# Where P1 + P6 is built in the layer-1 scores of a two-layer attention kernel

## The chip, the cores and the metric

The kernel runs on one core of a Trainium2 chip. A core has TensorE (matmuls, "PE" in the profile; its weight loads are "PEld"), VectorE ("DVE"), ScalarE ("ACT"), GpSimd ("POOL") and SyncE ("SP", which here only issues DMAs). Matmul results land in PSUM, everything else lies in SBUF. The metric is the device time of the launch in microseconds, the median of several runs.

## What is computed

Eight images of 512 channels by 1024 tokens go through two attention layers, all in float32. Layer 0 has eight heads. Layer 1 has one head over all 512 channels, and the change lies in its scores. Cut to that, the reference reads:

```python
xn = group_norm(x, gamma, beta)
q = conv1x1(xn, q_w, q_b).reshape(b, c, h * w).transpose(0, 2, 1)
k = conv1x1(xn, k_w, k_b).reshape(b, c, h * w)
v = conv1x1(xn, v_w, v_b).reshape(b, c, h * w).transpose(0, 2, 1)
attn = jax.nn.softmax(jnp.einsum('bqc,bck->bqk', q, k) * scale, axis=-1)
out = jnp.einsum('bqk,bkc->bqc', attn, v)
```

## The kernel before

**Stages.** The work is traced in Python as one straight program. For each image b from 1 on it does: layer 0's attention for b (`attention0`), the projection of b (`projection`, which also makes a list `stats` of twelve deferred statistics operations for layer 1's norm), then layer 1 of image b - 1: `layer1_scores` (the query side g), `layer1_rest` with `scores1_twice` (scores and exponentials), the values z and the product with the values (`values1`), and then layer 0's values, keys and queries of image b + 1. The last image's layer 1 takes another routine, `scores1`. So `scores1_twice` runs seven times.

**The scores as a fast matrix product, twice over.** In `scores1_twice` the 1024 x 1024 scores are split into 2 x 2 blocks C11, C12, C21, C22 and computed with Winograd's form of Strassen's scheme: seven products P1 to P7 in place of eight, and

- C11 = P1 + P2
- U2 = P1 + P6, U3 = U2 + P7
- C12 = U2 + P5 + P3, C21 = U3 + P4, C22 = U3 + P5

Each product is computed by the same scheme again (`inner_steps`): seven inner steps in the order 1, 6, 2, 5, 7, 3, 4. An inner step is two matmuls of 128 x 128 weights by 256 columns; in float32 the profile shows four matmul records for it. Three PSUM banks a, b and c (two buffers each, so `psa`, `psb`, `psc` in the profile) hold the inner sums. Step 1 fills bank a, and ScalarE copies it into a new bank b (L459). Steps 6, 7 and 4 accumulate onto b, step 2 onto a, step 5 opens c and step 3 accumulates onto it. Between two accumulations onto the same bank, a partial sum is read out: u2 after step 6, c5 after step 5, the inner block (1,1) after step 7. VectorE does this reading with `add` (L720: PSUM plus an SBUF block into SBUF), or ScalarE with a copy (L449) where the product has nothing to add. So VectorE must have read a bank before TensorE may do the next step on it.

Steps 3 and 4 of a product are put off (`tail`) and are done after step 1 of the next product. Within a product the inner blocks are written in the order (0,0) by step 2, (1,1) by step 7, (0,1) by step 3, (1,0) by step 4.

**The seven products.** `product(s, p, y, x, before, small, after7, final)` is called in the order P1, P2, P5, P6, P7, P3, P4. It computes Pp, adds the block at place `x` (if any) and writes to place `y`; (0,1) is C12, (1,0) is C21, (1,1) is C22. `before` names the products whose query-side factors GpSimd builds at that point (`factors`, `query_factors`, four operations each, L426). `small` is a list of deferred operations that is appended to `background`; one of them is taken off after each inner step. They are: `gsteps`, sums of the query side on VectorE (L159 to L162); `stats`, eight `bn_stats` (L98) and four `bn_aggr` (L103) on VectorE; and `add_up`, sums of exponentials for the softmax on GpSimd (L731). `exps` are the exponentials in place on ScalarE (L727), two per block. `final` and `after7` put `exps` behind the last or the fifth inner step.

**The extra sums.** C22 holds P5 after the third product. U2 = P1 + P6 is written to C12's place; P7 reads U2 there and writes U3 to C21's place. In P7's product, `extra` (L746 to L752) then calls `more` (L722) twice for each inner block: when P7's add has read U2's block, C12 += C22 there (so C12 = U2 + P5), and when U3's block is written, C22 = U3 + P5. Six of these eight sums run on GpSimd, two on VectorE: C12's inner block (0,1) and C22's inner block (1,0). All are line L723, 128 x 512.

**What sets the order.** Each engine works off its own queue in order. A planner in the framework orders the instructions of each queue when the program is built; it may move an instruction ahead of others on its engine, while those wrapped in `tc.keep_in_program_order` keep their order among themselves. Matmuls, the factors on GpSimd (L426), `add_up` and `stats` are wrapped so; `add` and the old `more` are not. The framework also puts in all the waits, and it takes a buffer from a common pool of 32 tiles when a tile is first written.

Of the kernel before, what the change touches and what calls it, by code (L numbers as in the profile page):

```python
# [12 lines left out]
ALU = mybir.AluOpType  # L13
# [16 lines left out]
def two_attention_blocks_kernel(  # L30
# [8 lines left out]
    nc = tc.nc  # L39
# [26 lines left out]
    def matmul(*args, **kw):  # L66
        tc.keep_in_program_order(nc.tensor.matmul(*args, **kw))  # L67
# [97 lines left out]
    def right_sums(lo, hi, t124, sub):  # L165

        n = len(lo)
        t1, t2, t4 = ([f(j) for j in range(n)] for f in t124)
        b11, b12, b21, b22 = [l[0] for l in lo], [l[1] for l in lo], [h[0] for h in hi], [h[1] for h in hi]
        steps = [lambda j=j: sub(t1[j], b12[j], b11[j]) for j in range(n)]  # L170
        steps += [lambda j=j: sub(t2[j], b22[j], t1[j]) for j in range(n)]
        steps += [lambda j=j: sub(b12[j], b22[j], b12[j]) for j in range(n)]
        steps += [lambda j=j: sub(t4[j], b21[j], t2[j]) for j in range(n)]
        return {1: b11, 2: b21, 3: b22, 4: t4, 5: t1, 6: t2, 7: b12}, steps

    def main_path(ctx):
# [11 lines left out]
        def pair_tile(name):  # L188
            return big_tile(name, (P, 2, HT))
# [226 lines left out]
        def query_factors(f, uid):  # L416

            t = big_tile(f"inner_{uid}", (P, 4, 2 * P))
            s1, s2, s3, s4 = (t[:, i, :] for i in range(4))
            a11, a21, a12, a22 = (f[k][:, ts(i, 2 * P)] for k in range(2) for i in range(2))  # L420
            for dst, x, y, op in (
                (s1, a21, a22, ALU.add), (s2, s1, a11, ALU.subtract), (s3, a11, a21, ALU.subtract),
                (s4, a12, s2, ALU.subtract),
            ):

                tc.keep_in_program_order(nc.gpsimd.tensor_tensor(dst, x, y, op))  # L426
            return {1: a11, 2: a12, 3: s4, 4: a22, 5: s1, 6: s2, 7: s3}
# [273 lines left out]
        def scores1_twice(b, f, gf, gsteps, first, uid, stats):  # L701

            scale = C**-0.5
            e = {(c, cc, r): pair_tile(f"e_{uid}_{c}{cc}{r}") for r in range(2) for c in range(2) for cc in range(2)}
            total = pair_tile(f"sum_{uid}")
            parts = [pair_tile(f"sum{r}_{uid}") for r in range(2)]  # L710
            g2 = {1: first}

            def factors(p):
                g2[p] = query_factors(gf[p], f"{p}_{uid}")

            def blocks(at, r, cc):
                return [e[at[1], cc, at[0]][:, :, ts(r, 2 * P)]]

            def add(dst, ps, x):
                nc.vector.tensor_add(dst[0], ps, x[0])  # L720

            def more(engine, dst, x, y, r, cc):  # L722
                engine.tensor_tensor(blocks(dst, r, cc)[0], blocks(x, r, cc)[0], blocks(y, r, cc)[0], ALU.add)  # L723

            def exps(r, c):
                for cc in (1, 0):
                    nc.scalar.activation(e[c, cc, r], e[c, cc, r], AF.Exp, scale=scale)  # L727

            def add_up(r, c):

                on = lambda dst, x, y: lambda: tc.keep_in_program_order(nc.gpsimd.tensor_tensor(dst, x, y, ALU.add))  # L731
                if r == c:
                    return [on(parts[r], e[c, 0, r], e[c, 1, r])]
                return [
                    *(on(parts[r], parts[r], e[c, cc, r]) for cc in range(2)),
                    on(total[:, r, :], parts[r][:, 0, :], parts[r][:, 1, :]),
                ]

            def product(s, p, y, x, before, small, after7=(), final=()):
                def mm(ps, j, start):  # L740
                    for i in range(2):
                        matmul(
                            ps[:, i, :], f[p][j][:, ts(i, P)], g2[p][j], start=start and i == 0, stop=True, skip_group_check=True
                        )

                def extra(r, cc, read, written):  # L746
                    if p == 7:

                        if read:
                            more(nc.vector if (r, cc) == (0, 1) else nc.gpsimd, (0, 1), (0, 1), (1, 1), r, cc)  # L750
                        if written:
                            more(nc.vector if (r, cc) == (1, 0) else nc.gpsimd, (1, 1), (1, 0), (1, 1), r, cc)  # L752

                inner_steps(
                    f"{uid}_{s}", s % 2, 2, mm, add, lambda *at: blocks(y, *at), x and (lambda *at: blocks(x, *at)),
                    extra, after7, final, [lambda: background.extend(small), *(lambda q=q: factors(q) for q in before)],
                )

            product(0, 1, (1, 0), None, [2], stats[:3] + gsteps[:2])
            product(1, 2, (0, 0), (1, 0), [5], gsteps[2:4], (), [lambda: exps(0, 0)])  # L760
            product(2, 5, (1, 1), None, [6, 4], gsteps[4:])
            product(3, 6, (0, 1), (1, 0), [7, 3], add_up(0, 0) + stats[3:6])
            product(4, 7, (1, 0), (0, 1), [], stats[6:7])
            product(5, 3, (0, 1), (0, 1), [], stats[7:10], [lambda: exps(1, 1)], [lambda: exps(0, 1)])
            product(
                6, 4, (1, 0), (1, 0), [], stats[10:] + add_up(1, 1) + add_up(0, 1), (),
                [lambda: exps(1, 0), lambda: background.extend(add_up(1, 0) + steps)],
            )

            t = [[pair_tile(f"t{n}_{uid}_{cc}") for cc in range(2)] for n in (1, 2, 4)]  # L770
            engines = [nc.vector] * 4 + [nc.gpsimd] * 4
            fs, steps = right_sums(
                [(e[0, cc, 0], e[0, cc, 1]) for cc in range(2)], [(e[1, cc, 0], e[1, cc, 1]) for cc in range(2)],
                [lambda cc, n=n: t[n][cc] for n in range(3)],
                lambda *a: engines.pop(0).tensor_tensor(*a, ALU.subtract),
            )
            return total, {p: [x[:, i, :] for x in fs[p] for i in range(2)] for p in fs}
# [167 lines left out]
        def projection(b, af, xt, hooks=()):  # L945

            norm = GroupNorm(1, f"1_{b}", pinned=b > 0)
            stats, rest = [], []

            def residual(i, r, c, ps, u):  # L950
                oc = 2 * r + i
                xh = xt[oc][:, ts(c, HT)]

                tc.keep_in_program_order(
                    nc.vector.scalar_tensor_tensor(xh, ps, obias[0][:, oc : oc + 1], xh, ALU.add, ALU.add)
                )
                if (r, c) == (1, 1):

                    rest.append(lambda: tc.keep_in_program_order(nc.vector.tensor_add(xh, xh, u)))
                elif u is not None:  # L960
                    nc.vector.tensor_add(xh, xh, u)
                stats.append(lambda: norm.half_stats(oc, c, xh))

                if c == 1 - r:
                    stats.append(lambda: norm.end_stats(oc))

            def add_rest():
                for f in rest:
                    f()

            def store():
                spills[b] = spool.tile([KC, P, T], F32, tag="spill", name=f"spill_{b}")
                for c in range(KC):
                    nc.sync.dma_start(spills[b][c], xt[c])

            by_channel(
                weight("p"), af, f"p_{b}", residual, middle=(5, 6, 7, 2), hooks=[[], [], hooks, [], [add_rest]],
                after=[load_weight, store],
            )
            return norm, stats  # L980
# [69 lines left out]
        for b in range(B):  # L1050
# [33 lines left out]
            if b > 0:  # L1084
# [4 lines left out]
                norm1, stats = projection(b, af, xt, [scaled, steps[7]])  # L1089
                gf, gsteps = layer1_scores(b - 1, hf, inner)  # L1090
# [12 lines left out]
            elif B > 1:  # L1103
                v, f, norm0 = values(1, hf, [[], [], [], [], [*steps[:7], scaled, steps[7]]])
                norm1, stats = projection(0, af, xt)
# [3 lines left out]
            else:  # L1109
# [3 lines left out]
                norm1, stats = projection(0, af, xt)  # L1113
# [9 lines left out]
        gf, gsteps = layer1_scores(B - 1, hf, None)  # L1123
# [197 lines left out]
```

## Time and profile before

| | |
|---|---|
| median of 3 runs | 2895.41 us |
| lowest and highest run | 2894.38, 2897.06 us |
| the profiled execution, its own time | 2894.85 us |
| its span, first to last instruction | 2893.1 us |
| TensorE busy | 2847.5 us |
| VectorE, ScalarE, GpSimd busy | 2069.1, 919.8, 1092.1 us |
| mean granted TensorE clock over the span | 0.997 |

In the lines of the profile, "psc<-inner,h" is an operation that writes tile psc from tiles inner and h; "128x512 f32" is partitions by elements; "L720" is line 720 of the kernel; "x4" means that four instructions are merged into one line; and brackets give the time for which the engine had been idle before and what ended it. Times are microseconds from the span's start. A matmul's end is modelled, so starts are what to read.

### The profile page before, as it was taken

The numbers are of one execution on the slowest core, as the hardware profiler recorded it, in microseconds if no ns is written. First come the engines' busy times: TensorE is split into PE (matmuls) and PEld (weight loads), VectorE is DVE, ScalarE is ACT, GpSimd is POOL, SyncE is SP. The second block draws the span as 40 slices with busy tenths as digits, with TensorE's granted clock in tenths as the row PEclk, the third lists the DMA queues.
The fourth block names the chain that finished last, engine by engine and source line by source line (L and its number), as shares of the span: only waits on it lengthen the run. The fifth ranks groups of instructions, "written<-read, shape, count | busy, mean of one in ns | idle before, by whom it ended". The sixth has DMA issues, their size and how long they took to land.

```text
span 2893.1 us, 31974 instructions
## 1 busy us (share of the span) xinstructions
PE 2847.5 (98%) x11720; PEld 1669.2 (58%) x11720; DVE 2069.1 (72%) x2732; ACT 919.8 (32%) x1166; POOL 1092.1 (38%) x1096
## 2 busy tenths in 40 slices
PE   9999999999999999999999999999999999999998
PEld 5435636765367653667437674376733768347544
DVE  5587787667876678775787757877588775886654
ACT  1351452214522045221542215421163212633110
POOL 2113216632166322763227612376123661146200
PEclk9999999999999999999999999999999999999999
DMA  8722403133032221322212231122411223022201
GB/s 278 248 87 105 156 19 142 40 129 126 24 134 80 104 110 48 110 92 99 108 48 106 92 136 71 48 106 100 151 52 45 106 103 147 23 76 75 95 0 67
DMA packets 91594, 281.02 MB, mean 97 GB/s; under 512 B 10595, under 2 KB 36387, under 8 KB 82470
## 3 DMA queue, kind: packets, MB, share of 16 engines
q1 hardware_dynamic: 89638, 276.61, 26.1%
q10 hardware_dynamic: 1792, 2.29, 0.2%
q8 instruction: 95, 1.56, 0.2%
q14 instruction: 69, 0.57, 0.1%
HBM read 225.93 MB, written 52.93 MB: 96 GB/s over the span
## 4 chain that ended last, share of the span: by engine, by line
PE 93%; issue 2%; DVE 2%; POOL 2%; DMA 0%; SPq 0%; ACT 0%; DVEq 0%; POOLq 0%
PE sc L67 16%; PE av L67 16%; PE psb_av L67 6%; PE psa_av L67 4%; PE psc_av L67 4%; PE psb L67 3%; PE psb_z L67 3%; PE psb_p L67 3%; PE psb_v L67 3%; PE psb_g L67 3%; PE psb_k L67 3%; PE psb_q L67 2%; PE psc L67 2%; PE psa_p L67 2%; PE psa_z L67 2%
## 5 line engine op out<-in xcount | busy, mean ns | idle before, releaser
L625 DVE TENSOR_TENSOR sum<-sum,e 128x1024 f32<-128x1024 f32 x384 | 520.2, 1355 | 41.8 <-ACT e L621 1.4
L621 ACT ACTIVATE e<-sc 128x1024 f32<-128x1024 f32 x512 | 476.9, 1053 | 73.1 <-PE sc L67 72.3
L67 PE MATMUL sc<-q,k 64*128 64x512 f32 x2048 | 458.7, 596 | 0.5
L67 PE MATMUL av<-e,v 128*64 128x512 f32 x2048 | 453.6, 595 | 0.0
L67 PEld LDWEIGHTS sc<-q,k 64*128 64x128 f32 x2048 | 193.2, 186 | 239.2 <-ACT e L621 104.0
L67 PEld LDWEIGHTS av<-e,v 128*64 128x64 f32 x2048 | 141.4, 137 | 304.3 <-issue 304.3
L588 POOL TENSOR_TENSOR all_recs<-all_recs,rc 128x256 f32<-128x256 f32 x72 | 63.6, 883 | 574.4 <-DVE rc L586 566.7
L644 POOL TENSOR_TENSOR a<-a,r 128x512 f32<-128x512 f32 x56 | 112.6, 2010 | 262.0 <-DMA r<-rows 262.0
L586 DVE RECIPROCAL rc<-sums 128x256 f32<-128x256 f32 x72 | 126.5, 1756 | 47.5 <-PE sums L67 26.5
L639 ACT COPY a<-av 128x512 f32<-128x512 f32 x64 | 37.5, 585 | 322.6 <-PE av L67 322.6
L532 POOL TENSOR_TENSOR k<-k,k 128x256 f32<-128x256 f32 x28 | 20.1, 728 | 314.0 <-DVE u_k L527 314.0
L623 DVE TENSOR_TENSOR sum<-e,e 128x1024 f32<-128x1024 f32 x64 | 78.5, 1226 | 59.2 <-ACT e L621 59.2
L67 PE MATMUL psa_av<-e,z 128*128 128x512 f32 x256 | 113.3, 595 | 0.0
L140 ACT ACTIVATE h<-h,b,s 128x1024 f32<-128x1024 f32 x62 | 78.4, 1269 | 86.8 <-DMA h<-in_x 70.1
L67 PE MATMUL psb<-inner,inner_h 128*128 128x256 f32 x392 | 104.5, 390 | 0.8
L411 POOL TENSOR_TENSOR inner_h<-h,inner_h 128x256 f32<-128x256 f32 x112 | 101.4, 908 | 2.2
L67 PEld LDWEIGHTS psb<-inner,inner_h 128*128 128x128 f32 x392 | 75.9, 196 | 16.1 <-POOL inner L426 3.4
L727 ACT ACTIVATE e<-e 128x1024 f32<-128x1024 f32 x56 | 58.2, 1054 | 78.9 <-POOL e L723 36.9
L731 POOL TENSOR_TENSOR sum<-sum,e 128x1024 f32<-128x1024 f32 x28 | 65.9, 2354 | 43.5 <-ACT e L727 42.4
L67 PEld LDWEIGHTS psa_av<-e,z 128*128 128x128 f32 x256 | 48.0, 190 | 57.3 <-issue 56.6
L411 POOL TENSOR_TENSOR inner_h<-h 128x256 f32<-128x256 f32 x56 | 54.3, 969 | 66.7 <-ACT h L140 66.7
L411 POOL TENSOR_TENSOR inner_h<-t_h 128x256 f32<-128x256 f32 x84 | 74.0, 884 | 12.9 <-PE psc_av L67 8.8
(383 smaller groups left out, 5463.6 us busy)
## 6 DMA issues: line engine op xcount, KB each, us to landing
x<-in_x SPq DMA_DIRECT2D x36, 512.0 KB
h<-in_x SPq DMA_DIRECT2D x32, 512.0 KB
spill<-x SPq DMA_DIRECT2D x32, 512.0 KB
h<-spill SPq DMA_DIRECT2D x32, 512.0 KB
x<-spill SPq DMA_DIRECT2D x32, 512.0 KB
out<-x SPq DMA_DIRECT2D x64, 256.0 KB
w_p<-sums_p SPq DMA_DIRECT2D x8, 1792.0 KB
r<-rows SPq DMA_DIRECT2D x112, 128.0 KB
```

The source lines that it names most:

```text
L67: tc.keep_in_program_order(nc.tensor.matmul(*args, **kw))
L140: tc.keep_in_program_order(nc.scalar.activation(dst, src, AF.Identity, bias=b, scale=s))
L411: pin(nc.gpsimd.tensor_tensor(dst, x, y, ALU.subtract))
L586: nc.vector.reciprocal(rc, sums)
L588: nc.gpsimd.tensor_tensor(all_recs, all_recs, rc, ALU.add)
L621: nc.scalar.activation(e, sc, AF.Exp, scale=(C // 8) ** -0.5)
L623: nc.vector.tensor_add(total, es[0], e)
L625: nc.vector.tensor_add(total, total, e)
L639: nc.scalar.copy(dst, av)
L644: nc.gpsimd.tensor_tensor(dst, dst, r, ALU.mult)
L727: nc.scalar.activation(e[c, cc, r], e[c, cc, r], AF.Exp, scale=scale)
L731: on = lambda dst, x, y: lambda: tc.keep_in_program_order(nc.gpsimd.tensor_tensor(dst, x, y, ALU.add))
```

## The change

U2 = P1 + P6 is now built in C21's place, where P1 already lies, so P6's adds work in place. `more` takes no engine any more: it always runs on GpSimd and keeps its program order there. When a block of U2 is written (in P6's product), C12 = U2 + P5 is computed from C21's place and C22 into C12's place. P7 then works in place on C21, which becomes U3, and when a block of it is written, C22 = U3 + P5 is computed as before. So GpSimd does all eight sums, four in P6's product and four in P7's.

The deferred operations are spread anew: the second group of statistics (two `bn_stats` and one `bn_aggr`) moves from P6's product to P5's, the later ones move forward accordingly, and `add_up(0, 0)` moves from P6's product to P3's.

```diff
-            def more(engine, dst, x, y, r, cc):
-                engine.tensor_tensor(blocks(dst, r, cc)[0], blocks(x, r, cc)[0], blocks(y, r, cc)[0], ALU.add)
+            def more(dst, x, y, r, cc):
+
+                tc.keep_in_program_order(
+                    nc.gpsimd.tensor_tensor(blocks(dst, r, cc)[0], blocks(x, r, cc)[0], blocks(y, r, cc)[0], ALU.add)
+                )
...
                 def extra(r, cc, read, written):
-                    if p == 7:
-
-                        if read:
-                            more(nc.vector if (r, cc) == (0, 1) else nc.gpsimd, (0, 1), (0, 1), (1, 1), r, cc)
-                        if written:
-                            more(nc.vector if (r, cc) == (1, 0) else nc.gpsimd, (1, 1), (1, 0), (1, 1), r, cc)
+
+                    if p == 6 and written:
+                        more((0, 1), (1, 0), (1, 1), r, cc)
+                    if p == 7 and written:
+                        more((1, 1), (1, 0), (1, 1), r, cc)
...
             product(0, 1, (1, 0), None, [2], stats[:3] + gsteps[:2])
             product(1, 2, (0, 0), (1, 0), [5], gsteps[2:4], (), [lambda: exps(0, 0)])
-            product(2, 5, (1, 1), None, [6, 4], gsteps[4:])
-            product(3, 6, (0, 1), (1, 0), [7, 3], add_up(0, 0) + stats[3:6])
-            product(4, 7, (1, 0), (0, 1), [], stats[6:7])
-            product(5, 3, (0, 1), (0, 1), [], stats[7:10], [lambda: exps(1, 1)], [lambda: exps(0, 1)])
+            product(2, 5, (1, 1), None, [6, 4], gsteps[4:] + stats[3:6])
+            product(3, 6, (1, 0), (1, 0), [7, 3], stats[6:7])
+            product(4, 7, (1, 0), (1, 0), [], stats[7:9])
+            product(5, 3, (0, 1), (0, 1), [], stats[9:11] + add_up(0, 0), [lambda: exps(1, 1)], [lambda: exps(0, 1)])
             product(
-                6, 4, (1, 0), (1, 0), [], stats[10:] + add_up(1, 1) + add_up(0, 1), (),
+                6, 4, (1, 0), (1, 0), [], stats[11:] + add_up(1, 1) + add_up(0, 1), (),
                 [lambda: exps(1, 0), lambda: background.extend(add_up(1, 0) + steps)],
             )
```

## The prediction

> **What bounds the kernel now.** I read the page first. TensorE is busy nearly all the time, and the chain that ended last runs over it.
>
> ```profile
> PE 2847.5 (98%) x11720; PEld 1669.2 (58%) x11720; DVE 2069.1 (72%) x2732; ACT 919.8 (32%) x1166; POOL 1092.1 (38%) x1096
> PE 93%; issue 2%; DVE 2%; POOL 2%; DMA 0%; SPq 0%; ACT 0%; DVEq 0%; POOLq 0%
> ```
>
> No change to another engine is worth anything unless TensorE stands somewhere for it. So the second view is the list of waits, for TensorE alone (total, times, longest).
>
> ```profile
> PE psc L67 <- DVE mv L103: 24.2, 7, 3.7
> PE psb L67 <- DVE e L720: 5.0, 7, 0.7
> ```
>
> Both come seven times: once for each of the seven images that take the twice-split scores (the eighth takes another routine). Everything else on that list is under 5 us together, outside this stage. The third view is the timeline of image 0 around the long wait, engine by engine; TensorE first (start, length, instruction).
>
> ```profile
> 529.98 1.03 PE L67 MATMUL psa<-g,t_h 128*128 128x256 f32 x4
> 534.41 1.50 PE L67 MATMUL psc<-inner,h 128*128 128x256 f32 x4 [3.41 <-DVE mv L103]
> 535.71 1.91 PE L67 MATMUL psb<-sg,inner_h 128*128 128x256 f32 x4
> 537.42 1.51 PE L67 MATMUL psb<-inner,inner_h 128*128 128x256 f32 x4
> 538.77 1.03 PE L67 MATMUL psa<-g,t_h 128*128 128x256 f32 x4
> ```
>
> One inner step is four matmul records and 0.865 us start to start. The step that stands is P3's inner step 3 (it comes after P4's inner step 1). It accumulates onto bank c, so VectorE must first have read the c5 sum out of that bank.
>
> ```profile
> 527.65 0.69 DVE L720 TENSOR_TENSOR u<-psb,e 128x512 f32<-128x512 f32 x1 [0.24 <-PE psb L67]
> 531.78 0.69 DVE L723 TENSOR_TENSOR e<-e,e 128x512 f32<-128x512 f32 x1 [3.44 <-POOL e L723]
> ...
> 533.60 0.67 DVE L720 TENSOR_TENSOR c<-psc,e 128x512 f32<-128x512 f32 x1
> ```
>
> The c5 read at 533.60 was late only because VectorE stood 3.44 us in front of L723, its own C22 sum of P7, waiting for GpSimd. (The list names mv L103, a small operation just behind c5 that ended last.) And GpSimd:
>
> ```profile
> 517.64 0.73 POOL L426 TENSOR_TENSOR inner<-sg,inner 128x256 f32<-128x256 f32 x1
> 518.33 2.35 POOL L731 TENSOR_TENSOR sum<-e,e 128x1024 f32<-128x1024 f32 x1
> 524.11 7.64 POOL L723 TENSOR_TENSOR e<-e,e 128x512 f32<-128x512 f32 x6 [3.43 <-issue]
> ```
>
> GpSimd was free at 520.68, began its six sums at 524.11 and needed 7.64 us for them. What it waited for is VectorE's P7 sum at 523.30 to 523.97, which reads U2 out of C12's place: only then may L723 overwrite C12. So the chain is P7's read, six sums, VectorE's sum, c5, TensorE. All seven images have it, 3.4 to 3.7 us.
>
> **What the Trainium skill says.** On its page "TensorE: Matmul & The Clock Gate", section "What's actually happening": after an idle window of about 3.4 us the array runs at half clock until a busy window has passed. The trace agrees: after the stall the three steps take 4.36 us (534.41 to 538.77); in image 6, which kept its clock, the same three take 2.66 (2659.95 to 2662.61). The granted clock over this stage (the windows view) reads 0.96 in five images and 1.00 in two. The Trainium skill's page "SBUF — State Buffer", section "Who interferes with whom": a VectorE tensor_tensor with two SBUF inputs contends with a GpSimd operation that reads SBUF; with one SBUF input it does not. The trace agrees: L426 on GpSimd takes 0.73 us alone and 1.06 to 1.24 beside VectorE's sums L159 to L162, while L723 kept 1.27 beside L720, which reads PSUM. The Trainium skill's page "Perfetto Trace Analysis", section "Tensor Engine Instruction": the queues of VectorE, ScalarE and GpSimd are strict FIFO. Agreed: L720 operations with data ready stood behind L723.
>
> **The change, part by part** (image 0; other images have the same pattern).
>
> *C12's sums one product earlier.* They now need P6's writes into C21's place. In the old trace VectorE ends those at about 518.0, 519.2, 519.9 and 521.1, the last three behind statistics that move away, so they will be earlier. GpSimd's queue before them: the factors for P7 and P3, eight operations of L426 that end at 518.33. From there four sums of 1.27 end at 519.6, 520.9, 522.1 and 523.4. P7's four sums follow when VectorE has written them (about 521.9, 524.8, 525.4, 526.2): they end near 524.6, 525.9, 527.2, 528.4. GpSimd gets 8 sums for 6, 2.5 us more work; its cover is its idle time (3.43 us before the sums and 1.89 and 3.5 us after them).
>
> *VectorE loses two sums* of 0.69 (0.60 in the queue), and with them its only wait on GpSimd in the stage, 3.44 us. TensorE's 24.2 us go, and with them the half clock: 5 times (4.36 - 2.66 = 1.70) = 8.5 us.
>
> *P7's adds in place.* Their number, shape and 0.69 us stay. They gain a new wait: each may overwrite a block of C21 only when GpSimd's P6 sum has read it. Behind each are VectorE's c5 and the bank reads for which TensorE would stop. Due times against GpSimd's ends: 521.2 against 519.6, 524.1 against 520.9, 524.7 against 522.1, 525.6 against 523.4. The least margin is 1.6 us, so I cost it at 0. P3's adds read C12: first at 526.7 against 522.1.
>
> *The exponentials of C22* (two L727, 1.06 each) stand on ScalarE ahead of the copy that opens P4's bank b (0.58). GpSimd's ends give exponentials at 527.3 and 528.5 to 529.6; the copy can go at once when TensorE's step 1 of P4 ends, near 530.1, and TensorE needs it near 531.7. Cost 0, margin about 1.5 us of lateness on GpSimd. This is what is late next.
>
> *add_up(0,0)* (2.35 on GpSimd) moves from P6's product to P3's, behind the eight sums: 528.4 to 530.8. add_up(1,1) then ends near 533.1, and the exponentials of C12, for which the next sums wait, near 533.7. These all move with TensorE, so 0. In its old place it would delay the sums by 2.35.
>
> *Statistics.* Two L98 (0.60 in the queue) and one L103 go from P6's product to P5's; the other L98 and L103 move one product or a slot earlier. In P5's product and at P6's start VectorE idles 1.15, 0.97 and 1.09 us between its adds, so two times 0.60 fit: cost 0 to 0.3 us per image, I take 0. In P6's product they made the P7-step add late for which inner step 4 stands 0.7 us (519.28): that wait goes, 5.0 us. No DMA is moved; SP only may load into freed image tiles sooner.
>
> *Sum:* 24.2 + 8.5 + 5.0 = 37.7 us. Against the profiled execution's own 2894.85 (span 2893.1 and 1.75 around it) that is 2857.2; the median of the runs is 0.56 above that execution, so 2857.7. Small late starts (0.16 us at 524.72) may add 1 us of gain, 0.3 us of new lateness in P5 takes 2.
>
> **Rivals.**
>
> *A shorter wait takes the place of the old.* If the planner leaves add_up(0,0) ahead of the sums, or VectorE's sums stretch GpSimd's to 1.84 (1.27 times 1.06/0.73), GpSimd is 2.35 or 8 x 0.57 = 4.6 us late; less the margin of 1.5, TensorE stands 0.85 to 3.1 us per image on ScalarE's copy, too short for the clock to fall: 6 to 22 us are given back, 2864 to 2879. For it: the margin is small. Against: the six sums ran at 1.27 with VectorE busy beside them.
>
> *Nothing is won.* At 2.01 us each, as L644 takes for 128x512 in the attention, eight sums are 5.9 us late: 4.4 us of stall seven times is 31, the half clock comes back (8.5): 2897. Against: L644 runs beside VectorE's two-SBUF sums L625; here, after L162 (over by 509.7), VectorE's only such operations were L723 itself, which leaves.
>
> *Slower.* One mechanism: GpSimd is late enough that VectorE and ScalarE both wait for it in their queues. With the sums at 2.01 and the eight factors at 1.2 instead of 0.73 it is 5.9 + 3.8 = 9.7 us late: 8.2 us of stall seven times (57) and seven clock drops (12) against 37.7 saved: 2927. It decides from 1.5 + (37.7 - 8.5)/7 = 5.7 us of lateness. Against: the factors of P7 and P3 ran at 0.73 in this very place.
>
> **Chances.** Main 0.78 (2853 to 2861), shorter wait 0.12, nothing 0.05, slower 0.05. Measurement tells about 0.2%, 6 us; so faster 0.90, same 0.05, slower 0.05. The range runs from 2853 to 2868: it takes in the margin case of 0.85 us and half of the shorter waits.
>
> **What would show it.** Right: TensorE's wait on mv L103 and on e L720 gone from the list; L723 only on GpSimd, 56 times at 1.27, in two groups of four, the first starting near 518.4; the clock 1.00 over the stage in all seven images; the stage of 46.9 us near 41. Wrong: a wait of TensorE's psb on ScalarE's L459, L723 above 1.5 us, or VectorE's L720 waiting for GpSimd.

## The result and the profile after

The changed kernel takes **2853.11 us** (median of 4 runs, 2852.44 to 2853.79); the kernel before, run beside it, 2896.23 us (4 runs, 2894.38 to 2898.99). The ratio is 0.985, 95% interval 0.9833 to 0.9867: 43.1 us less, where 37.7 were forecast. The profiled execution took 2852.44 us and its span is 2850.6, 42.5 less than before.

The page's first lines for the changed kernel: busy times, and the chain that ended last.

```profile
PE 2834.5 (99%) x11720; PEld 1665.7 (58%) x11720; DVE 2062.8 (72%) x2718; ACT 919.9 (32%) x1166; POOL 1106.2 (39%) x1110
PE 98%; issue 1%; DVE 1%; POOL 0%; ACT 0%; DVEq 0%; POOLq 0%
```

VectorE has 14 instructions fewer and GpSimd 14 more, two per image. GpSimd's share of the chain is gone, and TensorE's rose from 93% to 98%. The list of TensorE's waits now begins so (total, times, longest):

```profile
PE tr_wk L70 <- DMA rawk<-in_w: 4.1, 2, 3.7
PE psa_v L67 <- POOL h L142: 0.8, 1, 0.8
```

Both lines that came seven times are gone; what is left lies outside the scores. The timeline of TensorE in image 0, at the place of the old stand (after P4's inner step 1, the psa line):

```profile
529.24 1.03 PE L67 MATMUL psa<-g,t_h 128*128 128x256 f32 x4
530.10 1.03 PE L67 MATMUL psc<-inner,h 128*128 128x256 f32 x4
530.96 1.03 PE L67 MATMUL psb<-sg,inner_h 128*128 128x256 f32 x4
531.83 1.03 PE L67 MATMUL psb<-inner,inner_h 128*128 128x256 f32 x4
```

The steps are 0.86 us apart, no stand, no half clock. GpSimd and ScalarE in the same stretch:

```profile
518.80 9.87 POOL L725 TENSOR_TENSOR e<-e,e 128x512 f32<-128x512 f32 x8
528.63 4.69 POOL L734 TENSOR_TENSOR sum<-e,e 128x1024 f32<-128x1024 f32 x2
```

```profile
528.71 1.06 ACT L730 ACTIVATE e<-e 128x1024 f32<-128x1024 f32 x1 [0.17 <-POOL e L725]
530.30 0.57 ACT L459 COPY psb<-psa 128x512 f32<-128x512 f32 x1 [0.53 <-PE psa L67]
```

(Line numbers have moved: L725 is the old L723, L730 the old L727, L734 the old L731.) All eight sums run in one row, 1.23 us apart, straight behind the factors. The copy L459 waits for TensorE, with 0.53 us to spare.

**Where the 42.5 us came from.** Starts of matmuls, not the list of waits, give the full account. In the kernel before, image 0 went from P2's inner step 1 at 497.66 to the first matmul of the values at 541.36: 43.70 us. The changed kernel goes from 498.14 to 535.28: 37.14 us. That is 6.56 us less in this image. Beside the long stand, TensorE is late at two places in the old trace, at P6's inner step 4 and at P7's tail:

```profile
517.54 1.03 PE L67 MATMUL psc<-inner,t_h 128*128 128x256 f32 x4
519.28 1.13 PE L67 MATMUL psb<-sg,inner_h 128*128 128x256 f32 x4 [0.71 <-DVE e L720]
520.24 1.03 PE L67 MATMUL psb<-inner,inner_h 128*128 128x256 f32 x4
...
523.70 1.03 PE L67 MATMUL psa<-sg,h 128*128 128x256 f32 x4
524.72 1.10 PE L67 MATMUL psc<-inner,h 128*128 128x256 f32 x4
525.66 1.03 PE L67 MATMUL psb<-g,inner_h 128*128 128x256 f32 x4
```

With an undisturbed step of 0.865 us, the old trace has, above that pace: 0.97 us at P6's inner step 4 and the step after it; 0.23 at P7's tail (the late start at 524.72 and the step after it); 3.57 at P3's inner step 3 and about 0.07 after it; and 1.70 for the half clock. Without the clock this is 4.84 us an image; seven times that, 0.3 more in image 1 and five times 1.70 make 42.7. Added up over the seven images, the stretch took 302.8 us before and takes 260.0 after.

### The profile page after: what moved, and what is told of

Read it like the earlier page. It is cut to its first block, busy times and chain, and to the rows that moved or that the text cites. A ratio compares the mean times of both kernels' runs of the same rounds, so it can differ in the third digit from the quotient of the medians.

```text
span 2850.6 us, 32020 instructions
## 1 busy us (share of the span) xinstructions
PE 2834.5 (99%) x11720; PEld 1665.7 (58%) x11720; DVE 2062.8 (72%) x2718; ACT 919.9 (32%) x1166; POOL 1106.2 (39%) x1110
## 3 DMA queue, kind: packets, MB, share of 16 engines
q1 hardware_dynamic: 89638, 276.61, 26.5%
## 4 chain that ended last, share of the span: by engine, by line
PE 98%; issue 1%; DVE 1%; POOL 0%; ACT 0%; DVEq 0%; POOLq 0%
PE sc L67 16%; PE av L67 16%; PE psb_av L67 6%; PE psb L67 5%; PE psa_av L67 4%; PE psc_av L67 4%; PE psc L67 3%; PE psa L67 3%; PE psb_z L67 3%; PE psb_p L67 3%; PE psb_v L67 3%; PE psb_g L67 3%; PE psb_k L67 3%; PE psb_q L67 2%; PE psa_p L67 2%; PE psa_z L67 2%
## 5 line engine op out<-in xcount | busy, mean ns | idle before, releaser
L67 PE MATMUL psb_g<-inner_h,w_m 128*128 128x256 f32 x294 | 75.1, 383 | 0.3
L67 PE MATMUL psb_q<-inner_h,w_q 128*128 128x256 f32 x294 | 75.4, 385 | 0.0
```

## The experiments

Nine kernels. Each is compared with runs of the kernel before on the same chip, whose medians were 2896.6 to 2897.0; the changed kernel is 2853.1. It was not run again beside them, so a difference of about 1 us from it says little by the medians alone.

**e1_engine: the engine, U2 left in C12's place.** The kernel before with all eight sums on GpSimd, in program order.

```diff
...
-                            more(nc.vector if (r, cc) == (0, 1) else nc.gpsimd, (0, 1), (0, 1), (1, 1), r, cc)
+                            more((0, 1), (0, 1), (1, 1), r, cc)
                         if written:
-                            more(nc.vector if (r, cc) == (1, 0) else nc.gpsimd, (1, 1), (1, 0), (1, 1), r, cc)
+                            more((1, 1), (1, 0), (1, 1), r, cc)
```

(`more` itself is that of the changed kernel.)

> The kernel before with one part of the change: all eight extra sums on GpSimd in program order; U2 still in C12's place, deferred operations as before. If the place of U2 is what counts (my theory): GpSimd still waits for P7's reads, starts near 522.1 in image 0 and ends its eight sums near 532; VectorE no longer waits, but ScalarE's exponentials of C22 do, and with them the copy that opens P4's bank b, so TensorE stands some 1.3 us per image there instead of 3.6, without the half clock; about 2870 us. If freeing VectorE's queue of its wait is all there is to it: the full gain, about 2855. If the engine means nothing: 2896.

Measured: 2872.16 us, ratio 0.9913 (0.9897 to 0.993). In its trace (TensorE, then ScalarE, image 0):

```profile
533.55 1.13 PE L67 MATMUL psb<-inner,inner_h 128*128 128x256 f32 x4 [1.52 <-ACT psb L459]
```

```profile
531.96 1.06 ACT L730 ACTIVATE e<-e 128x1024 f32<-128x1024 f32 x1 [1.53 <-POOL e L725]
532.92 0.58 ACT L459 COPY psb<-psa 128x512 f32<-128x512 f32 x1
```

VectorE's wait has turned into ScalarE's: the second exponential waits for GpSimd, the copy stands behind it in the queue, and TensorE stands for the copy. This is the wait that the first rival named, and it is shorter than the old one (1.52 us, 1.81 in image 6) and leaves the clock alone. The short stand at P6's inner step 4 is still there in all seven images, 5.0 us by the list. So taking VectorE's two sums away, with the fixed order on GpSimd, is worth 24.8 us, but not the whole. The fixed order was not tried apart from the engine.

**e2_spread: only the new places of the deferred operations.** Statistics and add_up(0,0) as in the changed kernel, all else as before.

```diff
-            product(2, 5, (1, 1), None, [6, 4], gsteps[4:])
-            product(3, 6, (0, 1), (1, 0), [7, 3], add_up(0, 0) + stats[3:6])
-            product(4, 7, (1, 0), (0, 1), [], stats[6:7])
-            product(5, 3, (0, 1), (0, 1), [], stats[7:10], [lambda: exps(1, 1)], [lambda: exps(0, 1)])
+            product(2, 5, (1, 1), None, [6, 4], gsteps[4:] + stats[3:6])
+            product(3, 6, (0, 1), (1, 0), [7, 3], stats[6:7])
+            product(4, 7, (1, 0), (0, 1), [], stats[7:9])
+            product(5, 3, (0, 1), (0, 1), [], stats[9:11] + add_up(0, 0), [lambda: exps(1, 1)], [lambda: exps(0, 1)])
             product(
-                6, 4, (1, 0), (1, 0), [], stats[10:] + add_up(1, 1) + add_up(0, 1), (),
+                6, 4, (1, 0), (1, 0), [], stats[11:] + add_up(1, 1) + add_up(0, 1), (),
```

> The kernel before with the other part alone: statistics and add_up(0,0) spread as in the changed kernel, the extra sums and U2's place as before. My theory: TensorE's short stand at P6's inner step 4 goes (0.98 us start to start, seven times, and 0.23 at P7's tail), 8 us; GpSimd still waits for P7's read and VectorE for GpSimd, some 2.8 to 3.4 us per image; 2876 if the stand is now too short for the half clock, 2887 if it is not. Rival (add_up(0,0) ahead of GpSimd's sums was the cause): 2855.

Measured: 2902.37 us, ratio 1.0024 (1.0015 to 1.0033). Both expectations missed; it is slower than before. TensorE's stand at P6's inner step 4 did go, but the long one grew to 4.94 us, and the trace has the half clock in all seven images. VectorE's line says why, beside GpSimd's:

```profile
529.88 2.81 DVE L723 TENSOR_TENSOR e<-e,e 128x512 f32<-128x512 f32 x1 [2.85 <-POOL e L723]
```

```profile
522.21 7.64 POOL L723 TENSOR_TENSOR e<-e,e 128x512 f32<-128x512 f32 x6 [4.18 <-DVE e L720]
529.80 2.34 POOL L731 TENSOR_TENSOR sum<-e,e 128x1024 f32<-128x1024 f32 x1
```

VectorE's sum takes 2.81 us instead of 0.69. It starts just after GpSimd began add_up(0,0), which in this kernel stands right behind the six sums, and it ends at 532.69, half a microsecond after GpSimd's operation. Both read two operands from SBUF. All seven images have it.

**e9_spread_stats: the statistics spread, add_up(0,0) left in P6's product.** It was made to test that reading.

```diff
-            product(3, 6, (0, 1), (1, 0), [7, 3], stats[6:7])
+            product(3, 6, (0, 1), (1, 0), [7, 3], add_up(0, 0) + stats[6:7])
...
-            product(5, 3, (0, 1), (0, 1), [], stats[9:11] + add_up(0, 0), [lambda: exps(1, 1)], [lambda: exps(0, 1)])
+            product(5, 3, (0, 1), (0, 1), [], stats[9:11], [lambda: exps(1, 1)], [lambda: exps(0, 1)])
```

(The minus lines are those of e2_spread.)

> The kernel before with only the statistics spread as in the changed kernel; add_up(0,0) stays in P6's product, ahead of GpSimd's sums, and U2 in C12's place. It parts two readings of e2_spread, where VectorE's sum L723 took 2.81 us instead of 0.69 while GpSimd ran add_up(0,0). If the two contend (both read two operands from SBUF), L723 takes 0.69 again, VectorE's wait for GpSimd is about 2.9 us, TensorE's stand about 3 us and seldom long enough for the half clock: 2877 to 2885. If the spread statistics themselves made the stand longer: about 2902 again.

Measured: 2879.7 us, ratio 0.9936 (0.9919 to 0.9952). VectorE and GpSimd in its trace:

```profile
529.97 0.69 DVE L723 TENSOR_TENSOR e<-e,e 128x512 f32<-128x512 f32 x1 [2.85 <-POOL e L723]
```

```profile
522.30 7.64 POOL L723 TENSOR_TENSOR e<-e,e 128x512 f32<-128x512 f32 x6 [1.84 <-issue]
531.83 2.35 POOL L731 TENSOR_TENSOR sum<-e,e 128x1024 f32<-128x1024 f32 x1 [1.89 <-ACT e L727]
```

The same sum at the same place, behind the same wait of 2.85 us, takes 0.69 us once GpSimd has nothing right behind its sums. So GpSimd's operation beside it was the cause. Between the two kernels only that operation of 2.35 us moved, by two products, and the medians lie 22.7 us apart. In the profiled executions, start to start, the stage is 20.7 us longer in e2_spread: 14.6 for the longer stands and 6.0 for the half clock (3 images here, 7 in e2_spread, where it costs 1.4 to 1.7 us each).

**e3_place and e4_addup: the changed kernel with deferred operations put back.** e3_place puts all of them back, e4_addup only add_up(0,0):

```diff
-            product(3, 6, (1, 0), (1, 0), [7, 3], stats[6:7])
+            product(3, 6, (1, 0), (1, 0), [7, 3], add_up(0, 0) + stats[6:7])
...
-            product(5, 3, (0, 1), (0, 1), [], stats[9:11] + add_up(0, 0), [lambda: exps(1, 1)], [lambda: exps(0, 1)])
+            product(5, 3, (0, 1), (0, 1), [], stats[9:11], [lambda: exps(1, 1)], [lambda: exps(0, 1)])
```

> The changed kernel with the deferred operations put back where they were before (add_up(0,0) and the statistics in P6's product); U2 in C21's place, all sums on GpSimd. GpSimd's sums then start 2.35 us later and end near 531.0; the exponentials of C22 keep ScalarE until 532.1, so the copy for P4's bank b ends 0.85 us after TensorE could use it: 7 x 0.85 = 6 us over the changed kernel, 2859. If the statistics in P6's product still hold inner step 4 there, TensorE is later itself and hides this: 2860 all the same. Rival (the new spread does most of it): 2870 or more.

> The changed kernel with add_up(0,0) alone put back into P6's product, ahead of the sums on GpSimd: a lateness of 2.35 us for all eight sums and nothing else. By the margin of 1.5 us that the prediction gave, TensorE stands about 0.85 us per image at P4's inner step 6, waiting for ScalarE's copy L459: 6 us, 2859. If GpSimd's lateness is hidden anyway: 2853.

Measured: e3_place 2858.16 us, ratio 0.9866 (0.985 to 0.9883); e4_addup 2858.58, ratio 0.9868 (0.9851 to 0.9884). e3_place differs from e1_engine only in where U2 is built, and so in when C12's sums come: that alone is worth 14.0 us. Against the changed kernel both cost the same 5.0 to 5.5 us, so with U2 in its new place the statistics' new places are worth nothing that shows, and add_up(0,0)'s is worth about 5. TensorE in e4_addup:

```profile
523.69 1.10 PE L67 MATMUL psc<-inner,h 128*128 128x256 f32 x4 [0.22 <-DVE mv L103]
...
531.88 1.13 PE L67 MATMUL psb<-inner,inner_h 128*128 128x256 f32 x4 [0.18 <-ACT psb L459]
```

2.35 us of lateness on GpSimd show as two short waits: one through VectorE at P7's tail, where an add in place (e<-psa at 521.66) waited 0.86 us for GpSimd's P6 sum, and one through ScalarE's copy. (In e3_place it is one wait, 0.62 to 0.65 us, for the copy.) 5.5 us over seven images are 0.78 each: a margin of 1.57 us. Start to start the trace shows 0.91 in each image, a margin of 1.44.

**e5_late1 and e6_late4: more work ahead of P7's sums.** C12's last inner block is computed two times in e5_late1 and five times in e6_late4, with the same values. The edit of e5_late1 (e6_late4 has 5 in place of 2):

```diff
-                        more((0, 1), (1, 0), (1, 1), r, cc)
+                        for _ in range(2 if (r, cc) == (1, 0) else 1):
+                            more((0, 1), (1, 0), (1, 1), r, cc)
```

> The changed kernel with one sum more on GpSimd per image: C12's last inner block is computed twice (same values). It makes the later four sums 1.25 us late. Margin 1.5 us: nothing is lost, 2853, within 1 us. If there is no margin: 1.25 x 7 = 9 us, 2862.

> The changed kernel with four sums more on GpSimd per image: C12's last inner block is computed five times (same values). The sums of C22 come 5.0 us late. Less the margin of 1.5: TensorE stands 3.5 us per image at P4's inner step 6, or earlier at P7's step 4 add, 24.5 us; if so long a stand also brings the half clock in some of the images, 1.7 us each, up to 12 more: 2878 to 2890. A stand that is only as long as before without the half clock would tell that the clock needs something else.

Measured: e5_late1 2853.16 us, ratio 0.9849 (0.9836 to 0.9862): 1.25 us of lateness cost nothing. e6_late4 2879.59, ratio 0.9943 (0.9928 to 0.9957): 26.5 us for 5 us of lateness, 3.8 per image. TensorE in e6_late4, image 0 and then image 1:

```profile
529.77 1.97 PE L67 MATMUL psb<-inner,inner_h 128*128 128x256 f32 x4 [2.06 <-DVE u L720]
531.53 1.89 PE L67 MATMUL psa<-g,t_h 128*128 128x256 f32 x4
...
881.75 1.10 PE L67 MATMUL psb<-inner,inner_h 128*128 128x256 f32 x4 [2.07 <-DVE u L720]
...
886.83 1.13 PE L67 MATMUL psb<-inner,inner_h 128*128 128x256 f32 x4 [1.32 <-ACT psb L459]
```

The first stand is the new wait of the adds in place (VectorE behind GpSimd, 3.28 us in its own queue), the second the copy. In images 0, 5 and 6 the clock halved after the first stand; there the second is absent, since the slow steps take up its time: the stretch takes 41.13 us in image 0 and 41.11 in image 1. So here the half clock cost almost nothing.

**e7_two_dve: two of the eight sums back on VectorE, U2 in C21's place.**

```diff
-            def more(dst, x, y, r, cc):
-
+            def more(dst, x, y, r, cc, engine=nc.gpsimd):
                 tc.keep_in_program_order(
-                    nc.gpsimd.tensor_tensor(blocks(dst, r, cc)[0], blocks(x, r, cc)[0], blocks(y, r, cc)[0], ALU.add)
+                    engine.tensor_tensor(blocks(dst, r, cc)[0], blocks(x, r, cc)[0], blocks(y, r, cc)[0], ALU.add)
                 )
...
-                        more((0, 1), (1, 0), (1, 1), r, cc)
+                        more((0, 1), (1, 0), (1, 1), r, cc, nc.vector if (r, cc) == (0, 1) else nc.gpsimd)
                     if p == 7 and written:
-                        more((1, 1), (1, 0), (1, 1), r, cc)
+                        more((1, 1), (1, 0), (1, 1), r, cc, nc.vector if (r, cc) == (1, 0) else nc.gpsimd)
```

> The changed kernel with two of the eight sums back on VectorE (C12's inner block (0,1) and C22's (1,0), as before the change), U2 in C21's place. If the place of U2 did it and not the engine: VectorE has 1.2 us more per image and no wait for GpSimd, for the block it adds to was read by GpSimd long before; 2853, within 2 us. If the engine did it: most of the 43 us come back.

Measured: 2854.29 us, ratio 0.9854 (0.9839 to 0.9868), 1.2 us over the changed kernel. That is near the noise, but the trace bears it out: start to start the stretch takes 37.36 or 37.37 us in each image, against 37.14 or 37.15. VectorE's two sums:

```profile
518.73 0.81 DVE L724 TENSOR_TENSOR e<-e,e 128x512 f32<-128x512 f32 x1
...
525.71 0.93 DVE L724 TENSOR_TENSOR e<-e,e 128x512 f32<-128x512 f32 x1
```

They now run while GpSimd does its own, and take 0.81 and 0.93 us in place of 0.69. So the place of U2, with the deferred operations where the change puts them, brings nearly everything; the engine is then worth about 1 us, though in the old place (e1_engine) it was worth 24.8. The new place with nothing else changed was not run.

**e8_pin_g: a further step.** The changed kernel with the query side's sums kept in program order.

```diff
-                [lambda j, t=t: t[:, j, :] for t in stiles], nc.vector.tensor_add, nc.vector.tensor_sub,
+                [lambda j, t=t: t[:, j, :] for t in stiles],
+                *(
+                    (lambda *a: tc.keep_in_program_order(nc.vector.tensor_add(*a)),
+                     lambda *a: tc.keep_in_program_order(nc.vector.tensor_sub(*a)))
+                    if inner else (nc.vector.tensor_add, nc.vector.tensor_sub)
+                ),
```

(`inner` holds for the seven images with twice-split scores.)

> The changed kernel with the query side's eight sums (gsteps) kept in program order, one after each inner step, where the planner now runs them in pairs back to back. In the changed kernel TensorE still loses 0.83 us per image in P2's and P5's products (start to start over 42 steps: 37.14 us against 36.31), while VectorE is behind pairs of these sums. If the pairs are the cause, up to 6 us go: 2847 to 2850. If GpSimd's factors, which wait for these sums, come too late instead: slower, 2855 to 2865.

Measured: 2849.1 us, ratio 0.9835 (0.9822 to 0.9848): 4.0 us under the changed kernel, the fastest of all. VectorE in the changed kernel, and then in e8_pin_g:

```profile
500.82 2.03 DVE L160 TENSOR_TENSOR sg<-sg,g 128x512 f32<-128x512 f32 x2
502.77 0.68 DVE L720 TENSOR_TENSOR u<-psb,e 128x512 f32<-128x512 f32 x1
```

```profile
502.05 0.69 DVE L720 TENSOR_TENSOR u<-psb,e 128x512 f32<-128x512 f32 x1 [0.95 <-PE psb L67]
502.66 0.77 DVE L1026 TENSOR_TENSOR sg<-sg,g 128x512 f32<-128x512 f32 x1
```

In place of two sums back to back, u2 is read as soon as TensorE has written it. TensorE's late starts in P2's and P5's products fall from 0.83 us per image to 0.33 in image 0 and 0.30 to 0.31 in the others, 3.7 us over seven images.

## Where the prediction held, and the term that was too small

*C12's sums one product earlier: right.* The first was due near 518.4 and ran at 518.80, in a trace that is 0.48 us later here; the last was due to end at 528.4 and ended at 528.67. They ran in one row, where two groups of four were expected. e1_engine shows what the engine leaves, and its comparison with e3_place what the place adds.

*VectorE's wait for GpSimd, TensorE's stand and the half clock: right.* All are gone, and the clock over the stage reads 1.00 in all seven images.

*The size: 5 us too small, and here the prediction failed.* The failed term of the sum is "24.2 + 5.0", taken from the list of waits. That list counts from the modelled end of the last matmul, 1.03 us after its start, while steps follow each other at 0.865; each stand is thus 0.16 us longer than listed, and the step behind it starts up to 0.10 late. Two stands in seven images make 2.3 and 1.2 us, so the term is 32.7 and not 29.2. The late start at P7's tail was put at 1 us of possible gain and left out of the sum; start to start it is 0.23 us, 1.6 in all. Together 5.1: 37.7 becomes 42.8, against 42.5 in the span. The range, 2853 to 2868, was drawn for losses on the upper side; its lower end left no room for this. It counted from a kernel before of 2895.41 us, so it allowed for a gain of 42.4 at most; beside a kernel before of 2896.23 the gain was 43.1. By its bare numbers the range holds 2853.11, by 0.1 us; that is luck.

*The new wait of the adds in place, cost 0: right.* So was the margin: 1.5 us given, nothing lost at 1.25 (e5_late1), 0.8 to 0.9 us per image at 2.35 (e4_addup). What is late next is both waits that were named, VectorE's and ScalarE's, within a few tenths of each other.

*add_up(0,0): right.* In its old place it costs 5 to 5.5 us; 6 were worked out. What the prediction did not see is that the same move without U2's new place costs time (e2_spread).

*Statistics: the effect right, the cause half right.* The stand at P6's inner step 4 went, as forecast. But spreading the statistics (e2_spread, e9_spread_stats) and writing in place (e3_place, statistics where they were) each take it away alone; that the statistics stood there was thus not the whole cause. In the kernel before, VectorE did P6's step-2 add (517.34) behind c5 (516.01) and a statistic, though TensorE does step 2 ahead of step 5; in e3_place it comes before both. Why the planner put it so was not tried.

*The rivals.* The shorter wait in its place is what e1_engine and e4_addup show. "Nothing won" and "slower" needed GpSimd's sums at 2.01 us; they ran at 1.27.

## What to carry to other kernels

When an in-order engine waits for another one's row of operations, ask which single read holds the first of them: writing an intermediate where its last ingredient already lies can take that read away. Here, once that was done and the deferred operations spread, it mattered by only 1 us which engine did two of the sums. Price a stand of TensorE from start to start of its matmuls against the undisturbed pace, since a list of waits leaves out what lies under a modelled end. And give a new order a margin in microseconds of lateness, then measure it by adding work: here 1.25 us were free and 2.35 were not.

## What was not expected of the hardware

A VectorE sum with two operands in SBUF took 2.81 us instead of 0.69 because GpSimd had begun an operation of 2.34 us with two SBUF operands 0.08 us earlier (e2_spread), and 0.69 again with GpSimd idle (e9_spread_stats). In the changed kernel VectorE's L720 adds, with one operand in PSUM and one in SBUF, kept 0.69 us beside the same operation (529.68 and 531.16, GpSimd busy from 528.63 to 533.32). The Trainium skill states such a lock ("SBUF — State Buffer", section "Who interferes with whom"), and this agrees with it; the prediction had used it only against GpSimd.

The half clock also came after stands shorter than the 3.4 us for which the prediction took it. By the list of waits: 1.5 to 1.8 us (e1_engine), in none of seven images; 2.06 (e6_late4), in three; 2.8 to 3.1 (e9_spread_stats), in three; 3.4 to 3.7 (before), in five; 4.9 to 5.0 (e2_spread), in seven. The length of the stand does not decide alone: in e9_spread_stats the longest, 3.12 us in image 1, brought no half clock, and three of 2.82 to 2.84 did. "TensorE: Matmul & The Clock Gate", section "What's actually happening", in the Trainium skill speaks of an idle window of about 3.4 us; the measurement decides, and here a stand of 2 us was enough in some images. What in those images made the difference was not tried.
